# Making Q and K two batches ahead, and dealing the first batch's pieces from two lists

## The chip, the cores and the metric

The kernel runs on one core of one Trainium2 chip. The time is device microseconds of one execution. Three runs of the kernel before are shown: 2144.08, 2147.13 and 2149.2 us, median 2147.13. A core has engines with a queue each: TensorE (PE, its weight loads shown as PEld), VectorE (DVE), ScalarE (ACT), GpSimd (POOL) and SyncE (SP), which here only issues DMAs.

## What is computed

One transformer layer in float32 with post-norm: 8 sequences ("batches") of 1024 rows, width 256, 16 heads of 16, a hidden layer of 1024.

```python
def attention(x):                       # x: (8, 1024, 256)
    Q, K, V = (split_heads(x @ W.T + b) for W, b in ((Wq, bq), (Wk, bk), (Wv, bv)))
    scores = einsum('bhqd,bhkd->bhqk', Q, K) / sqrt(16)
    scores = scores + prior_lambda * gaussian_mask(1024)
    out = einsum('bhqk,bhkd->bhqd', softmax(scores), V)
    return merge_heads(out) @ Wo.T + bo

def ffn(x):
    h = bitlinear(x, w_fc) + gate * (x @ v.T @ fast_b.T @ u.T)
    return bitlinear(relu(h) ** 2, w_proj)     # bitlinear: weights to -1, 0, 1 times a row's mean

x = layernorm(x + attention(x))
out = layernorm(x + ffn(x))
```

## The kernel before

**Groups.** The whole attention is a loop over 512 groups (`for g in range(-LEAD, total + 1)`), 64 to a batch. One group works on two heads' pairs of one block of 128 rows. Its fixed part, in PE's order: the scores transposed for the exps (`exp_scores`, L761, into a tile `e`), some pieces of other work, the scores for the row maxima 12 groups later (`max_scores`, L665, tile `s`), the weighing of the values by the exps of the group before (`weigh`, L791), and matmuls that put the prior into the next `e` (`prior_scores`, L742) where the block lies near the diagonal. DVE reduces each `s` to row maxima (L677), ACT takes the exps (L776), and `e` and `s` share three buffers in PSUM (`se`). The first 12 groups, numbered -12 to -1 (the lead), only take maxima and make what batch 0 needs.

**Pieces.** All else is cut into pieces, each a tuple of cost, function, room in the two halves of the one PSUM bank `misc`, and a test whether it may run. A piece issues its matmuls at once and returns a function that empties the bank, issued after the scores of the maxima. In these texts they are called
- T: two transposes of x (`transpose_x`, L558), eight to a batch; after the fourth the second half of x is loaded into the same tile
- V: a block of the values (`values`, L584), eight to a batch
- Q: a quarter of Q or K of one half of the heads, c = 0 or 1 (`queries_keys`, L611), sixteen to a batch. Every second one is followed on ACT by a cast into the single buffer `two` (L630), a subtraction on POOL (L631), and `write_parts` (L201 to L206), SP's DMAs that write the pair to DRAM (`parts_k`, `parts_q`)
- P, t, L, H, O: output projection, transposes, low rank, hidden layer and output of the feed-forward, in four chunks, 68 to a batch
- weight pieces of batch 0: `prepare_v` (L419, reads `v_sb`), `prepare_fc` (L445, L460, L493, L494) and `prepare_proj` (L531, L537); they make the ternary weights on POOL, and `rows` leaves POOL's low-rank factors in `ones_low`, which L494 turns.

**Which pieces in which batch.** `jobs_of(b)` makes the list for batch b: Q of c = 1 of this batch; T, V and Q of c = 0 of the next one; the feed-forward of the batch before; less the last `KEPT` = 8 pieces, which go to the next batch. 100 pieces in a steady batch. In batch 0 there is no feed-forward, and the weight pieces are mixed with those of batch 1 by `spread`. The lead holds 14 pieces: V of batch 0 and six of the Q pieces of its c = 1.

**Dealing.** In each group the loop takes pieces from the head of the list while there is room in `misc`, the head is ready, and the costs so far (`filled`) are at most 0.75; past that only when the batch is behind (`spare`, the groups left less those that the list still needs), judged more strictly in groups `near` the diagonal. In batch 0 it deals evenly by count instead (`behind`).

**Queues.** An order over all instructions of an engine is fixed at the end, so each engine, SP too, works in the order of the program text. `fill_stack(G)` (L316) is eight SP DMAs that bring Q and K of one group of four heads from DRAM back into the operand tiles `st_k` and `st_q`; it is called every 16 groups, one group of heads ahead, and for G = 1 in group -2. `load_later` (L349 to L353) follows it there and loads `v_sb`, `fast_b`, `u`, the gate and `bo`. `set_max` writes the row maxima to DRAM and back into `st_q` (L702, L709).

Of the kernel before, what the change touches and what calls it, by code (L numbers as in the profile page):

```python
# [37 lines left out]
LEAD = 12  # L38
# [5 lines left out]
def tile_postln_layer(  # L44
# [42 lines left out]
    p2 = ctx.enter_context(tc.tile_pool(name="p2", bufs=2))  # L87
    epool = ctx.enter_context(tc.tile_pool(name="epool", bufs=4))
    dpool = ctx.enter_context(tc.tile_pool(name="dpool", bufs=2, space=bass.MemoryType.DRAM))
    first = len(nc.cur_bb.bb.instructions)  # L90
    before = ExitStack()
    ps_0 = before.enter_context(tc.tile_pool(name="ps_0", bufs=8, space=bass.MemoryType.PSUM))
# [98 lines left out]
    parts_of, made = {}, {}  # L191

    def new_parts(name, b, c):
        parts_of[name, b, c] = dpool.tile(
            [P, 4, L], F32, tag=f"parts_{name}", name=f"parts_{name}_{b}_{c}"
        )
        return parts_of[name, b, c]
# [234 lines left out]
    def prepare_fc(half):  # L432

        n = NHC // 2
        st = {}

        def first():
            w = p1.tile([P, n, D], F32, tag="hi", name=f"fc_{half}")
            nc.sync.dma_start(w, w_fc[ts(half, n * P), :].rearrange("(c p) d -> p c d", p=P))
            st["w"] = w  # L440
            st["uT"] = p1.tile([R, HALF], F32, tag="x1T", name=f"uT_{half}")
            pus = [misc(f"pu_{half}_{k}") for k in range(2)]
            for k, pu in enumerate(pus):
                for i in range(2):
                    nc.tensor.matmul(  # L445
                        pu[:R, ts(i, P)],
                        u_sb[:, n * half + 2 * k + i, :],
                        ident,
                        start=True,
                        stop=True,  # L450
                    )

            def empty():
                for k, pu in enumerate(pus):
                    nc.scalar.copy(st["uT"][:, ts(k, D)], pu[:R, :])

            return empty

        def factor(i, out):
            nc.tensor.matmul(out, st["uT"][:, ts(i, P)], fb_sb, start=True, stop=True)  # L460

        def second():
            pf = misc(f"pf_{half}")[:, :R]
            factor(0, pf)
            return lambda: tern(0, pf)

        def tern(i, pf):
            w, hc = st["w"][:, i, :], n * half + i
            sc = s_fc[:, hc : hc + 1]
            scales(sc, w, D)  # L470
            ternary(w, sc, f"fc_{half}_{i}")
            full = p1.tile([P, R], F32, tag="lowf", name=f"lowf_{half}_{i}")
            nc.scalar.copy(full, pf)

            def rows():

                inv = p2.tile([P, 1], F32, tag="inv", name=f"inv_{half}_{i}")
                nc.vector.reciprocal(inv, sc)
                nc.gpsimd.tensor_scalar(full, full, inv, gate_c, op0=ALU.mult, op1=ALU.mult)
                low = ones_low[:, 1, :].rearrange("p (a b c r) -> p a b c r", a=2, b=2, c=2)  # L480
                for k in range(2):
                    src = full.unsqueeze(1).to_broadcast([P, 2, R])
                    nc.gpsimd.tensor_copy(low[:, k, 0].bitcast(F32R), src)
                    nc.gpsimd.tensor_sub(low[:, k, 1], src, low[:, k, 0])
                st["rows"] = i

            defer(1, rows)

        def piece(i):
            pw = misc(f"pw_{half}_{i}")  # L490
            pl = misc(f"pl_{half}_{i}")
            for dc in range(NDC):
                nc.tensor.transpose(pw[:, ts(dc, P)], st["w"][:, i, ts(dc, P)], ident)  # L493
            nc.tensor.transpose(  # L494
                pl[:, :P], ones_low[:, 1, :], ident
            )
            if i + 1 < n:
                factor(i + 1, pl[:, P : P + R])

            def empty():  # L500
                at = ts(n * half + i, P)
                nc.scalar.copy(wfT[:, :, at], pw.rearrange("p (c h) -> p c h", h=P))
                nc.scalar.copy(lowT[:, at], pl[:, :P])
                if i + 1 < n:
                    tern(i + 1, pl[:, P : P + R])

            return empty

        return [(0.5, first, 2), (0.3, second, 1)] + [
            (0.5, lambda i=i: piece(i), 2, lambda i=i: st.get("rows") == i) for i in range(n)  # L510
        ]

    def prepare_proj(i):
# [887 lines left out]

    over = []

    def first_x(b, main):

        for f, n in zip(first_chunk[b][0], (-8, -2)):
            main[n] = with_(f, main[n])
        return main

    def jobs_of(b):  # L1410


        qk = queries_keys(b, 1, misc)
        load, early_xv, ahead = [], [], []
        if b + 1 < B:
            load = [(0.0, lambda: load_x(b + 1, 0), 0)]
            xs, vs = transpose_x(b + 1, misc), values(b + 1, misc)
            early_xv, ahead = xs[:4] + vs[: NB // 2], xs[4:]
            ahead = ahead + queries_keys(b + 1, 0, misc) + vs[NB // 2 :]
        if b + 1 < B:  # L1420
            first_chunk[b] = chunk(b, 0, misc)
        if b == 0:
            main = [(0.3, prepare_v, 1)] + [u for i in range(2) for u in prepare_fc(i)]
            main += [u for i in range(D // P) for u in prepare_proj(i)]
            side = ahead[:12] + early_xv[4:] + ahead[12:]
            return load + qk + early_xv[:4], first_x(b, spread(main, side, 0.05, 0.9))
        old = [over[k : k + 2] for k in range(0, len(over), 2)] or [[]] * 4
        if ahead:
            t, q, v = ahead[:4], ahead[4:12], early_xv[4:] + ahead[12:]

            lead = [t[0], t[1], q[0], t[2], q[1], t[3], q[2], q[3], v[4], q[4], q[5]]
            at_end = [[q[6], q[7]], [v[5], v[6]], [v[7]], []]
            main = v[:4] + feed_forward(b - 1, misc, lead, at_end)
            t = early_xv[:4]
        else:

            old_o = old[2] + old[3]
            t, old[2:], lead = [()] * 4, [[], []], [qk[6], qk[7], *old_o]
            main, qk = feed_forward(b - 1, misc, lead), qk[:6]
            load = [(0.0, f, 0) for k in (2, 3) for f in (ends[k]["load"], ends[k]["bias"])]  # L1440
            for f, n in zip((ends[0]["load"], ends[0]["bias"]), (-8, -2)):
                main[n] = with_(f, main[n])
        t = [list(u for u in (k,) if u) for k in t]
        jobs = load + [qk[0], *old[0], qk[1], *old[1], *qk[2:4]]

        jobs += [*old[2], *t[0], qk[4], *t[1], *old[3], *t[2], qk[5], *t[3], *qk[6:]]
        over[:] = main[-KEPT:] if b + 1 < B else []
        main = main[:-KEPT] if b + 1 < B else main
        return jobs, first_x(b, main) if b + 1 < B else main

# [48 lines left out]
        *e0["H"][4:],  # L1501
    ]
    rest, es = None, {}
    jobs = [u for part in jobs_of(0) for u in part]

    v_first, qk_first, jobs[:7] = values(0, misc), jobs[1:7], jobs[:1]
    early = [u for two in zip(v_first, qk_first) for u in two] + v_first[6:]
    for g in range(-LEAD, total + 1):

        now = g  # L1510
        if g == -8:
            split_prior()
        if g == -2:
            fill_stack(1)
            load_later()
        if 0 <= g < total and g % per_batch == 0:
            if g:
                assert not jobs
                jobs = [u for part in jobs_of(g // per_batch) for u in part]
        if g == total - 7:  # L1520

            old, jobs = jobs, []
# [29 lines left out]
        if g < 0:  # L1552

            n = g + LEAD + 1 - (done >= QSTEP - 1)
            upto = 14 * n // (LEAD - 1)
            if halves == 2:
                work += [early.pop(0)[1] for _ in range(len(early) - 14 + upto)]
        elif g < total:
            left = per_batch - 1 - g % per_batch
            if g == 0:  # L1560
                among = len(jobs)
            if g < per_batch:

                behind = len(jobs) > among * (1 - (g + 1) / (per_batch - 3))
            else:

                spare = left - groups_for(jobs) if g < total - per_batch else 0
            while jobs and halves >= jobs[0][2] and ready(jobs[0]):
                cost = jobs[0][0]
                if g < per_batch:  # L1570
                    if not (cost == 0.0 or behind):
                        break
                    behind = len(jobs) - 1 > among * (1 - (g + 1) / (per_batch - 3))
                elif filled > 0.75 and not (spare < (-1 if near(g) else 2)):
                    break
                elif filled > 0.9 and cost > 0.9 and spare > -4:
                    break
                cost, piece, room = jobs.pop(larger(jobs) if halves == 1 and g >= per_batch else 0)[:3]
                filled += cost
                halves -= room  # L1580
                work.append(piece)
# [103 lines left out]
```

## Time and profile before

| | |
|---|---|
| median of three runs | 2147.13 us |
| the profiled execution, its time | 2146.07 us |
| its span | 2144.3 us |
| PE busy | 2073.6 us (97%), weight loads 1200.6 us (56%) |
| DVE, ACT, POOL busy | 73%, 67%, 43% of the span |
| DMA | 193.55 MB, mean 90 GB/s |
| mean granted clock of TensorE | 0.994 |
| group 0 of the loop begins | 61.3 us |
| batches 0, 1, 2 to 6, 7 take | 242.4, 254.2, 253.7 to 253.8, 253.6 us |
| after the loop (from 2080.4) | 63.9 us |

Batches are told apart in the trace by the starts of the L761 matmuls, four to a group. A busy PE is not PE at its peak, since a matmul's record also holds time in which it stands in the array's pipeline. A wait is shown in brackets behind an instruction: how long its engine stood idle before it, and what ended this. "SPq" is SP's issue of a DMA, not the transfer.

### The profile page before, as it was taken

What the parts mean: (1) busy time and instruction counts of PE and PEld (TensorE: products, weight loads), DVE (VectorE), ACT (ScalarE), POOL (GpSimd) and SP (SyncE); (2) the same over time, 40 slices, a digit from 0 to 9 for tenths busy, and PEclk for the clock granted to TensorE, in tenths of its full rate; (3) what the DMA queues carried; (4) which work ended last, traced back from release to release, by engine and by line L of the source; (5) the groups of instructions that cost most, each with busy time, mean ns of one, the idle gap of its engine ahead of it and who ended that gap; (6) DMA issues with size and microseconds to landing.
All of it is one profiled execution on the core that took longest, in us unless ns stands there. A gap on an engine that the chain in (4) does not pass through costs nothing.

```text
span 2144.3 us, 38970 instructions
## 1 busy us (share of the span) xinstructions
PE 2073.6 (97%) x14200; PEld 1200.6 (56%) x14200; DVE 1568.2 (73%) x2909; ACT 1440.2 (67%) x2155; POOL 917.2 (43%) x1075
## 2 busy tenths in 40 slices
PE   6999999999999999999999999999999999999997
PEld 3444445555555555556555555555555555555657
DVE  6777777777777777777777777777777777777736
ACT  2566666766777667667777767677676766766754
POOL 5044332344324453345533445335543445455444
PEclk9999999999999999999999999999999999999999
DMA  6423334223433124423233223422343321422010
GB/s 192 124 76 112 77 88 143 68 62 78 124 103 107 56 60 121 137 73 84 72 133 110 76 70 99 132 86 58 78 124 120 90 70 49 138 74 56 23 47 20
DMA packets 110725, 193.55 MB, mean 90 GB/s; under 512 B 21149, under 2 KB 50253, under 8 KB 110533
## 3 DMA queue, kind: packets, MB, share of 16 engines
q1 hardware_dynamic: 109116, 189.48, 31.3%
q8 instruction: 112, 1.84, 0.4%
q10 hardware_dynamic: 1416, 1.58, 0.2%
q14 instruction: 81, 0.66, 0.1%
HBM read 105.19 MB, written 85.69 MB: 89 GB/s over the span
## 4 chain that ended last, share of the span: by engine, by line
PE 80%; DVE 11%; POOL 3%; DMA 3%; issue 2%; ACT 1%; SPq 0%; DVEq 0%; POOLq 0%; ACTq 0%
PE e L761 22%; PE av L791 19%; PE s L665 16%; DVE junk L677 8%; PE misc L1065 5%; PE misc L611 4%; PE misc L1100 4%; PE misc L584 2%; PE misc L991 2%; PE e L742 1%; PE misc L1072 1%; DVE st L949 1%; DMA parts_k<-twok 1%; PE misc L1025 1%; PE misc L558 0%
## 5 line engine op out<-in xcount | busy, mean ns | idle before, releaser
L677 DVE CUSTOM_DVE_ANT_0 junk<-s,wide 128x1024 f32<-128x1024 f32 x1024 | 1249.1, 1220 | 484.1 <-PE s L665 440.5
L776 ACT ACTIVATE exp<-e 128x1024 f32<-128x1024 f32 x1024 | 1027.6, 1024 | 549.2 <-PE e L761 371.3
L761 PE MATMUL e<-st_q,st_k 66*128 66x512 f32 (+1 forms) x2048 | 618.0, 423 | 0.7 <-DMA st_q<-rows 0.4
L791 PE MATMUL av<-exp,v 128*17 128x512 f32 x4096 | 539.8, 598 | 0.0
L761 PEld LDWEIGHTS e<-st_q,st_k 66*128 66x128 f32 (+1 forms) x2048 | 344.0, 189 | 292.8 <-ACT exp L776 95.3
L665 PE MATMUL s<-st_k,st_q 64*128 64x512 f32 x2048 | 393.9, 446 | 40.1 <-DVE pm L677 25.9
L665 PEld LDWEIGHTS s<-st_k,st_q 64*128 64x128 f32 x2048 | 165.3, 185 | 172.3 <-DVE pm L677 88.6
L775 DVE TENSOR_TENSOR e<-e,wide 128x372 f32<-128x372 f32 (+2 forms) x376 | 190.1, 506 | 38.2 <-PE e L761 35.7
L1083 POOL TENSOR_TENSOR rl<-rl 128x512 f32<-128x512 f32 x112 | 116.7, 1042 | 234.1 <-ACT hi L1082 221.1
L791 PEld LDWEIGHTS av<-exp,v 128*17 128x17 f32 x4096 | 68.1, 95 | 185.7 <-issue 184.3
L742 PEld LDWEIGHTS <-ident_q 96*32 96x32 bf16 x2112 | 64.3, 97 | 162.9 <-issue 159.0
L1085 POOL TENSOR_TENSOR lo<-rl,hi 128x512 fp32r<-128x512 f32 x112 | 143.8, 1284 | 8.8
L1120 POOL TENSOR_TENSOR r<-r,sp_row 128x256 f32<-128x256 f32 x56 | 41.1, 734 | 212.0 <-ACT r L1119 212.0
L594 POOL TENSOR_TENSOR v<-v,bv_row 128x256 f32<-128x256 f32 x64 | 44.0, 689 | 191.9 <-ACT v L593 191.9
L1065 PE MATMUL misc<-xhi,wfT 128*128 128x256 f32 x448 | 117.0, 284 | 0.4 <-ACT fullq L626 0.2
L1065 PE MATMUL misc<-xlo,wfT 128*128 128x256 f32 x448 | 115.0, 280 | 0.0
L1100 PE MATMUL misc<-wpT,lo 128*128 128x256 f32 x448 | 112.0, 282 | 2.6 <-POOL lo L1085 2.6
L1100 PE MATMUL misc<-wpT,hi 128*128 128x256 f32 x448 | 114.3, 288 | 0.0
L631 POOL TENSOR_TENSOR twok<-fullk,twok 128x512 fp32r<-128x512 f32 x30 | 38.6, 1287 | 145.3 <-ACT twok L630 143.6
L1078 ACT ACTIVATE rl<-misc,s_fc 128x256 f32<-128x256 f32 x224 | 94.0, 475 | 0.9 <-POOL lo L1085 0.9
L1065 PEld LDWEIGHTS misc<-xhi,wfT 128*128 128x128 f32 x448 | 84.4, 188 | 10.6 <-ACT fullk L626 2.4
L1100 PEld LDWEIGHTS misc<-wpT,lo 128*128 128x128 f32 x448 | 85.3, 190 | 6.7 <-POOL lo L1085 3.2
(233 smaller groups left out, 2351.9 us busy)
## 6 DMA issues: line engine op xcount, KB each, us to landing
st_k<-parts_k SPq DMA_DIRECT2D x128, 256.0 KB
st_q<-parts_q SPq DMA_DIRECT2D x124, 256.0 KB
parts_k<-twok SPq DMA_DIRECT2D x60, 512.0 KB
parts_q<-twoq SPq DMA_DIRECT2D x64, 256.0 KB
parts_q<-twoq SPq DMA_DIRECT2D x30, 512.0 KB
x<-in_L_attn_x_dram SPq DMA_DIRECT2D x16, 512.0 KB
raw_o<-avs SPq DMA_DIRECT2D x248, 32.0 KB
rec<-back SPq DMA_DIRECT2D x30, 256.0 KB
```

The source lines that it names most:

```text
L611: nc.tensor.matmul(pt, wT[name][:, dc, ts(c, P)], xT[:, dc, ts(2 * half + k, D)], start=(dc == 0), stop=(dc == NDC - 1),)
L665: nc.tensor.matmul(pair[a][:, kh, :], stack["q", s, pr, a][rows, ts(blk, P)], stack["k", s, pr, a][rows, ts(kh, HALF)], start=True, stop=True,
L677: nc.vector.tensor_tensor_reduce(out=junk, in0=t.rearrange("p k n -> p (k n)"), in1=wide[:, LEFT - P * blk : LEFT - P * blk + L], scale=1. ...
L761: nc.tensor.matmul(t[:, a, :], stack["k", s, pr, a][rows, ts(blk, P)], stack["q", s, pr, a][rows, ts(h, HALF)], start=not by_pe, stop=True ...
L775: nc.vector.tensor_add(part, part, add.to_broadcast([P, 2, hi - lo]))
L776: nc.scalar.activation(e, t.rearrange("p a n -> p (a n)"), AF.Exp)
L791: nc.tensor.matmul(av[32 * j : 32 * j + HD + 1, :], v_bufs[b % 2][:, blk, g * HG + j, : HD + 1], es[j // 2][:, ts(j % 2, HALF)], start=(n ...
L1065: nc.tensor.matmul(ph, wfT[:, dc, ts(hc, P)], st[k2][:, dc, :], start=(dc == 0 and k2 == "xhi"), stop=False,)
L1078: nc.scalar.activation(rl[:, ts(k, n)], ph, AF.Relu, scale=s_fc[:, hc : hc + 1])
L1083: nc.gpsimd.tensor_mul(rl, rl, rl)
L1085: sub(lo, rl, hi.bitcast(F32))
L1100: nc.tensor.matmul(py, st[k][:, hc, ts(i, P)], wpT[:, hc, :], start=(hc == 0 and k == "hi"), stop=(hc == NHC - 1 and k == "lo"),)
```

## The change

- `jobs_of(b)` now makes T and all 16 Q pieces of batch b + 2, and V of batch b + 1, beside the feed-forward of b - 1. Batch 6 so has no T and Q, batch 7 no T, Q and V; batch 6 leaves 12 pieces to batch 7 where the others leave 8.
- The `parts` tiles in DRAM come from a pool with six buffers for each name, where there were two.
- Batch 0 deals from two lists: `prepare` (weight pieces) and `side` (T, Q of batch 1, V of batch 1, T and Q of batch 2). Both are spaced evenly by count; after a weight piece a side piece still goes into the same group if the costs stay under 1.2 (1.1 near the diagonal). `prepare_v` is the first piece of group 0 (it was dealt in group 7).
- The lead now holds 20 pieces: all eight Q pieces of batch 0's c = 1 and four T pieces of batch 1. x of batch 1 is loaded when the loop starts (it was in group 0).
- A weight piece of `prepare_fc` waits one group more after `rows`.
- In later batches the rule for a second piece changes: -0.5 for -1 near the diagonal, no second piece past 0.4 while more than three groups are spare, and a fixed `spare` in the last batch.

```diff
-        parts_of[name, b, c] = dpool.tile(
+        parts_of[name, b, c] = dparts.tile(
...
-                st["rows"] = i
+                st["rows"], st["at"] = i, now
...
-            (0.5, lambda i=i: piece(i), 2, lambda i=i: st.get("rows") == i) for i in range(n)
+            (0.5, lambda i=i: piece(i), 2, lambda i=i: st.get("rows") == i and now > st["at"] + 1) for i in range(n)
...
-        qk = queries_keys(b, 1, misc)
...
+        v = values(b + 1, misc) if b + 1 < B else []
+        load, t, q0, q1 = [], [], [], []
+        if b + 2 < B:
+            load, t = [(0.0, lambda: load_x(b + 2, 0), 0)], transpose_x(b + 2, misc)
+            q0, q1 = queries_keys(b + 2, 0, misc), queries_keys(b + 2, 1, misc)
...
-            side = ahead[:12] + early_xv[4:] + ahead[12:]
-            return load + qk + early_xv[:4], first_x(b, spread(main, side, 0.05, 0.9))
+            side = transpose_x(1, misc) + queries_keys(1, 0, misc) + queries_keys(1, 1, misc)
+            return first_x(b, main, (-8, -2)), side + load + v + t + q0 + q1
...
+            lead = [t[4], t[5], q0[0], t[6], q0[1], t[7], *q0[2:]]
+            at_end = [q1[2:4], q1[4:6], q1[6:], []]
+            main = q1[:2] + feed_forward(b - 1, misc, lead, at_end)
+            t, v[6:] = [[u] for u in t[:4]], [v[6:]]
...
+            old += [[]] * (4 - len(old))
+            jobs = load + [v[0], *old[0], v[1], *old[1], *v[2:4]]
+            jobs += [*old[2], *t[0], v[4], *t[1], *old[3], *t[2], v[5], *t[3], *v[6]]
+        kept = KEPT if b + 2 < B else KEPT + 4
...
-    v_first, qk_first, jobs[:7] = values(0, misc), jobs[1:7], jobs[:1]
-    early = [u for two in zip(v_first, qk_first) for u in two] + v_first[6:]
+    early = [u for two in zip(values(0, misc), queries_keys(0, 1, misc)) for u in two]
+    early, side = early[:8] + side[:4] + early[8:], side[4:]
...
+        if g == -LEAD:
+            load_x(1, 0)
...
+        elif g < per_batch:
+            part = 1 - (g + 1) / (per_batch - 3)
+            while prepare and halves >= prepare[0][2] and ready(prepare[0]):
+                if filled > 0.1 or len(prepare) <= n_prepare * part:
+                    break
...
+            while side and halves >= side[0][2] and ready(side[0]):
+                cost = side[0][0]
+                if cost and (len(side) <= n_side * part - 3 or filled + cost > (1.1 if near(g) else 1.2)):
+                    break
...
-                elif filled > 0.75 and not (spare < (-1 if near(g) else 2)):
+                if filled > 0.75 and not (spare < (-0.5 if near(g) else 2)):
+                    break
+                elif filled > 0.4 and spare > 3:
                     break
```

## The prediction

> **What bounds the kernel now.** I read the batches first, as eight windows of the core's time (columns: stretch, us, then busy time of PE, weight loads, DVE, ACT and POOL, the granted clock, the DMA share and GB/s); the batches with numbers 0, 1, 5 and 7 are these:
>
> ```profile
> 61.30:303.73 242.43, 224.83 (x1518) 113.41 (x1513) 183.93 (x331) 153.68 (x220) 79.83 (x117) 0.99 0.31 84
> 303.73:557.90 254.17, 249.48 (x1706) 141.26 (x1701) 188.53 (x347) 175.22 (x260) 100.46 (x112) 1.00 0.33 93
> ...
> 1319.20:1573.00 253.80, 252.22 (x1758) 146.37 (x1752) 189.01 (x351) 179.29 (x269) 111.35 (x125) 1.00 0.33 94
> ...
> 1826.80:2080.41 253.61, 245.87 (x1721) 143.67 (x1715) 170.66 (x330) 173.88 (x250) 124.54 (x143) 1.00 0.25 69
> ```
>
> Batch 0 takes 242.4 us though PE stands idle for 17.6 us of it; the later ones take 253.8 with PE idle for 1.6. No other engine is near its limit. To price a moved piece I then took single groups, in the same columns: an empty one without and one with matmuls of the prior, one with a Q piece, one with Q and a transpose of x, one with two H pieces and the prior, one with an O piece.
>
> ```profile
> 289.14:292.70 3.56, 3.10 (x23) 1.29 (x17) 3.15 (x6) 2.05 (x2) 0.00 (x0) 1.00 0.02 5
> 296.38:300.05 3.67, 3.43 (x30) 1.60 (x24) 3.05 (x6) 2.05 (x2) 0.00 (x0) 1.00 0.03 9
> 303.73:307.37 3.64, 3.64 (x26) 1.87 (x21) 2.60 (x5) 2.41 (x3) 0.00 (x0) 1.00 1.05 225
> 1397.22:1401.10 3.88, 3.88 (x27) 2.04 (x22) 2.92 (x6) 2.62 (x4) 0.00 (x0) 1.00 0.00 0
> 1437.53:1441.59 4.06, 4.06 (x39) 2.74 (x34) 3.44 (x8) 2.52 (x4) 0.35 (x1) 1.00 0.03 8
> 1445.68:1449.40 3.72, 3.72 (x30) 2.21 (x24) 3.20 (x8) 2.50 (x3) 3.03 (x4) 1.00 1.04 226
> ```
>
> An empty group has a **floor** of 3.55 us (3.68 with the prior), from the three score buffers going round PE, DVE and ACT. A Q piece adds only 0.09; the next piece pays in full (+0.24 for the transpose). The rows fit: group = the larger of the floor and 2.77 (+0.13 prior) + pieces, at Q, V or P 0.865, T 0.23, L 0.48, H 0.6, O 0.95, row maxima 0.11. So 0.78 us of each group is free, and batch 0 leaves most of it unused. The Trainium skill (Perfetto Trace Analysis, section Identifying the Most-Contended Engine) says that matmul busy time is no measure of headroom. The page's 97% for PE would promise nothing for a refilled batch 0, the 0.09 us of the Q row promises nearly 0.8 per filled group; the rows decide, and the sum uses them alone.
>
> Last I read what PE waits for in batch 0, and the queue at its start.
>
> ```profile
> PE misc L494 <- POOL ones_low L484: 4.7, 6, 1.7
> ```
> ```profile
> 193.71 0.33 PE L494 MATMUL misc<-ident,ones_low 128*128 128x128 f32 x1 [1.67 <-POOL ones_low L484]
> ...
> 195.77 2.07 PE L761 MATMUL e<-st_q,st_k 66*128 66x512 f32 x4
> ...
> 197.64 1.61 PE L611 MATMUL misc<-xT,wqT 128*128 128x256 f32 x4
> ```
> ```profile
> 55.86 0.48 SPq L316 DMA_DIRECT2D st_k<-parts_k  x1
> ...
> 60.86 0.59 SPq L349 DMA_DIRECT2D v_sb<-in_L_ffn_v_dram  x1
> ...
> 65.51 0.38 SPq L201 DMA_DIRECT2D parts_k<-twok  x1
> ```
> ```profile
> 335.64 0.62 ACT L630 CAST twoq<-fullq 128x512 fp32r<-128x512 f32 x1 [1.34 <-DMA parts_k<-twok]
> ```
>
> Weight pieces wait for POOL. After the longest wait four e matmuls took 2.07 us instead of 1.20: the granted clock was 0.5 from 195.4 to 198.8, worth about 1.6 us. The Trainium skill (TensorE: Matmul & The Clock Gate, section What's actually happening) puts the half clock behind an idle window of about 3.4 us; here 1.67 us of wait came before it. By the page short waits would cost only themselves (4.7 us to be won from the weights); the row makes it 6.3, and I take the row. The last fence shows a cast that waits for the single `two` buffer, until the write of the pair before has landed.
>
> **The change, part by part.** The loop's rule, followed group by group with the readiness tests, gives the old order as the trace has it, and for the new one these tables' sums (old in brackets): batch 0 237.9 (234.1), batch 1 247.0 (246.3), each of 2 to 5 251.4 (250.3), batch 6 238.2 (250.3), batch 7 247.9 (251.1). The old batches took 8.3, 7.9, 3.5 and 2.5 more than their tables (0, 1, 2 to 6, 7): waits, which I carry over except where named.
>
> (1) Lead: x of batch 1 is loaded when the loop starts, in SP behind the fills that end at 40.4; a 512 KB write issued at 41.22 landed 2.7 us later, one at 41.65 3.6 later. The first T piece stands in group -8, which PE reaches at about 41.6, so x, at 43.1 to 44.9, is late. DVE's reduction pair of the next group stood at 43.00 and needs scores behind T: +2.0, from 0.5 to 3.5. No gain: reductions pace these groups at 1.38 each.
>
> (2) Groups 0 and 1: `prepare_v` moves from group 7 to 0, so PE wants v_sb at 62.4 and not at 89. The trace's completion events put the eight fills' landings at 59.4 to 68.1, one per 1.24 us, and v_sb's at 68.3, right behind them. Now the pair of K's second half is finished in group -3, ahead of fill_stack(1) in SP's order: V at 53.63 on PE, ACT held until 56.07 by the rows' DMA, then 0.37 + 0.47 + 0.62, POOL 1.29: 58.8. With two writes in front, fills start near 60 instead of 55.86 and v_sb lands near 73.4. PE waits 11 us; behind v_sb's matmuls stand T, the scores for DVE and all that follows. Two floor groups 7.2 + 11 + about 1 for the half clock, against 8.5 now: +10.7. Bounds: 0 (it lands in time) and +13.5 (two half-speed windows). Both shift with (1).
>
> (3) Batch 0 from group 2: table +3.9, for 26 more pieces; with one group more between rows and weight piece the 6.3 of L494 go. x's second half is loaded in group 41 and used in 42, 3.7 us later: +0.5. Q pieces run through 44 to 53 across the fill of group 48: the write of the cast in 49 queues behind some 13 us of fills, and the cast in 51 waits as in the last fence: +2.5 (0 to 4). Sum +0.6.
>
> (4) Batch 1: table 247.0, with the neighbours' 3.5 of waits and 1.5 for a cast behind the fill of group 16: 252.0, so -2.2 (-4 to +2).
>
> (5) Batches 2 to 5: the same 100 pieces, of which the last two groups get at most one: +1.1 by the table; the cast of group 18 after the one of 16 finds its buffer's write behind the fill: +0.8 (0 to 2). Four times 1.9: +7.6, from -2 to +14.
>
> (6) Batch 6: no transposes and no Q for a batch 8, four pieces more left over: 72 pieces for 100. Table -12.1; single H pieces leave POOL time, so waits fall from 3.5 to 2.5: -13.1 (-8 to -15.6).
>
> (7) Batch 7: eight Q pieces gone, four added, all in groups 0 to 11: table -3.2, and their casts' waits: -3.5 (-2 to -5). The tail is unchanged.
>
> Five more DRAM buffers and the new lists issue nothing. The DMA counts stay; only their order moves.
>
> Sum: 2.0 + 10.7 + 0.6 - 2.2 + 7.6 - 13.1 - 3.5 = **+2.1**. On the profiled execution's 2146.1 that is 2148.2; this execution lies 1.1 below the median of 2147.1 and inside the runs' 2144.1 to 2149.2.
>
> **The rivals.** *The start does not wait*: the small v_sb overtakes the fills and x comes in time. For: no instruction of before waited for either, and v_sb is 16 KB. Against: the completion order above. It takes 9 off (2) and 1 off (1): 2138. *Cast waits in every batch* (slower): runs of Q pieces, 15 to 23 in a steady batch, make a cast every two groups, 7.7 us; once a write needs longer from cast to landing, ACT holds the exps behind it. Group 72 of before shows the price: 4.68 us for a floor of 3.55. Two more per batch in 1 to 5 add 11.3: 2159.5. For: fills keep the queue for 12 us four times a batch; against: eight Q pieces running at 303.7 to 334 met one such wait. *Batch 6 does not shrink*: groups of one H stay near 3.95 through something not in my table, and (6) gives only 3: 2158. Against: the floor of 3.55 in batch 0.
>
> **How the numbers follow.** About 0.2% (4.3 us) is what a measurement tells from no change: same means 2142.8 to 2151.4. The forecast has chance 0.50, with its own range 2143 to 2154 (faster 0.05, same 0.33, slower 0.12 of it); the start that does not wait 0.25 (0.22 faster, 0.03 same); cast waits 0.19 (0.02 same, 0.17 slower); batch 6 0.06, slower. Together faster 0.27, same 0.38, slower 0.35. The range 2137 to 2160 reaches to both rivals and leaves out their outer halves.
>
> **What would show it.** Step (1): PE waits for x in the lead, near 42. (2): PE waits about 11 us for v_sb, with half clock after it. (3): no wait at the ones_low transpose; a cast wait near group 51. (5): batches 2 to 5 at about 255.7. (6): batch 6 near 240.7. (7): batch 7 near 250. The forecast is wrong if PE passes the v_sb matmuls at once, or if casts wait over 3 us per batch.

## The result, and the profile after

| | before | after |
|---|---|---|
| median, four runs of each side by side | 2148.11 us (2144.08 to 2149.20) | 2235.34 us (2235.14 to 2236.79) |
| ratio | | 1.0416, 95% interval 1.0403 to 1.0429 |
| span of the profiled execution | 2144.3 | 2233.5 |
| mean granted clock of PE | 0.994 | 0.976 |
| PE, DVE, ACT, POOL busy | 2073.6 us; 73%, 67%, 43% | 2105.1 us (94%); 70%, 64%, 41% |
| group 0 of the loop begins | 61.3 | 66.8 |
| batch 0, 1 | 242.4, 254.2 | 272.2, 259.0 |
| batches 2 to 5, each | 253.7 to 253.8 | 266.2 to 266.9 |
| batch 6, 7 | 253.8, 253.6 | 250.7, 254.7 |
| after the loop | 63.9 | 64.3 |

The changed kernel is 4.2% slower. The forecast was 2148.2 us with a range of 2137 to 2160. The spans differ by 89.2 us, and the table says where: 5.5 in the lead, 29.8 in batch 0, 4.8 in batch 1, 50.8 in batches 2 to 5, 1.1 in batch 7, 0.4 at the end, less 3.1 in batch 6.

The view of the batches as windows (stretch, us, then busy time of PE, weight loads, DVE, ACT and POOL, granted clock, DMA share, GB/s), for batches 0, 1, 5, 6 and 7 after the change:

```profile
66.84:339.00 272.16, 245.01 (x1614) 130.53 (x1608) 183.68 (x330) 169.50 (x258) 94.20 (x128) 0.94 0.39 118
339.00:598.00 259.00, 250.47 (x1707) 140.73 (x1701) 188.70 (x348) 175.78 (x260) 100.31 (x112) 0.99 0.34 95
...
1396.90:1663.80 266.90, 256.82 (x1758) 148.35 (x1752) 189.53 (x352) 178.99 (x268) 111.10 (x124) 0.99 0.32 89
1663.80:1914.50 250.70, 240.44 (x1660) 136.96 (x1652) 189.06 (x350) 164.18 (x230) 94.50 (x110) 0.99 0.22 54
1914.50:2169.20 254.70, 243.43 (x1710) 141.72 (x1703) 171.14 (x331) 170.42 (x243) 122.88 (x142) 0.99 0.22 56
```

Batch 5 shows the same 1758 PE entries as before, and its other engines are busy as long as before. PE now stands idle there for 10.1 us where it was 1.6. This waiting is 8.5 of the 13.1 us by which the batch grew; the other 4.6 are the same entries taking longer. In batch 0 it is 27.2 us, with a clock of 0.94.

One of these waits had been foreseen. The timeline of PE at the start of group 0 (start, us, engine, line, what, and in brackets the idle time before it and who ended it):

```profile
66.84 1.20 PE L762 MATMUL e<-st_q,st_k 66*128 66x512 f32 x4
78.84 1.00 PE L420 MATMUL misc<-ident,v_sb 16*128 16x16 f32 x4 [10.80 <-DMA v_sb<-in_L_ffn_v_dram]
```

PE waits 10.8 us for `v_sb`. Within this wait the clock fell to half and stayed there for 17 us, 9.2 of them behind the wait:

```profile
70.99:88.06 17.07, 9.02 (x30) 4.25 (x34) 4.52 (x11) 2.76 (x5) 0.00 (x0) 0.50 0.73 179
```

The large one had not. In each of batches 2 to 5, group 52 takes 11.3 to 12.6 us for a floor of 3.55. The timeline of batch 3 around it, first SP's queue (group 48 begins at 1058.05, group 52 at 1074.61):

```profile
1061.29 0.39 SPq L202 DMA_DIRECT2D parts_k<-twok  x1
...
1063.71 0.38 SPq L1115 DMA_DIRECT2D out_dram<-r  x1
1064.13 0.52 SPq L317 DMA_DIRECT2D st_k<-parts_k  x1
...
1068.54 0.59 SPq L317 DMA_DIRECT2D st_q<-parts_q  x1
1069.18 0.59 SPq L977 DMA_DIRECT2D x<-in_L_attn_x_dram  x1
...
1074.72 0.34 SPq L830 DMA_DIRECT2D den<-sums  x1
```

then the engines that need what stands at the end of that queue:

```profile
1076.55 1.40 POOL L983 TENSOR_TENSOR x<-x,bo_row 128x256 f32<-128x256 f32 x2 [10.50 <-DMA x<-in_L_attn_x_dram]
...
1078.25 0.55 DVE L835 RECIPROCAL den<-den 128x64 f32<-128x64 f32 x1 [3.41 <-DMA den<-sums]
...
1081.01 0.43 DVE L950 BATCH_NORM_STATS2 st<-r 128x6 f32<-128x256 f32 x1 [2.21 <-POOL r L1002]
...
1081.57 1.19 DVE L678 CUSTOM_DVE_ANT_0 junk<-s,wide 128x1024 f32<-128x1024 f32 x1
...
1082.82 1.29 PE L666 MATMUL s<-st_k,st_q 64*128 64x512 f32 x4 [5.84 <-DVE pm L678]
```

Read it from the end. PE waits 5.84 us for DVE's row maxima. DVE had nothing against them; they stand, in its order, behind the statistics of a norm, and those wait for POOL's residual `r`. POOL reaches `r` late since it waited 10.5 us, in its order, for a 256 KB piece of x to add a bias to. That piece was issued at 1069.18, behind the eight DMAs of `fill_stack` (2 MB). And the fill went out at 1064.13, 6.1 us after group 48 began, since two writes stood ahead of it on SP, each waiting for POOL: a K pair, and the store of a finished chunk. Before, the same queue read

```profile
998.03 0.50 SPq L316 DMA_DIRECT2D st_k<-parts_k  x1
...
1007.10 1.70 SPq L812 DMA_DIRECT2D raw_o<-avs  x4
...
1014.26 0.40 SPq L1114 DMA_DIRECT2D out_dram<-r  x1
```

with group 48 at 1001.61: the fill 3.6 us ahead of the group, the store 16 us behind the fill. The new lists end the O pieces of the chunk in group 45, where it was 47, and put a K pair into groups 46 and 47, where there was none. So both writes come in front of the fill. The P pieces that need x now stand in groups 50 and 51, where it was 52 and 53, so x is also wanted two groups sooner. This I shall call the order theory: SP, POOL and DVE each work in order, and one held entry on SP becomes, three queues on, a wait of PE.

### The profile page after: what moved, and what is told of

It reads as the page before. It is cut to its first block, busy times and chain, and to the rows that moved or that the text cites. A ratio compares the mean times of both kernels' runs of the same rounds, so it can differ in the third digit from the quotient of the medians.

```text
span 2233.5 us, 38927 instructions
## 1 busy us (share of the span) xinstructions
PE 2105.1 (94%) x14200; PEld 1219.3 (55%) x14200; DVE 1571.0 (70%) x2909; ACT 1439.6 (64%) x2155; POOL 915.9 (41%) x1075
## 4 chain that ended last, share of the span: by engine, by line
PE 63%; DVE 11%; DMA 3%; POOL 2%; ACT 1%; issue 1%; SPq 1%; DVEq 0%; POOLq 0%; ACTq 0%
PE e L762 17%; PE av L792 15%; PE s L666 13%; DVE junk L678 8%; PE misc L1066 4%; PE misc L1101 3%; PE misc L612 3%; PE misc L992 2%; PE misc L585 1%; DMA x<-in_L_attn_x_dram 1%; PE misc L1073 1%; PE e L743 1%; DVE st L950 1%; DVE xlo L1030 1%; SPq L317 1%
## 5 line engine op out<-in xcount | busy, mean ns | idle before, releaser
L762 PE MATMUL e<-st_q,st_k 66*128 66x512 f32 (+1 forms) x2048 | 624.6, 427 | 8.0 <-DVE pm L678 5.5
L792 PE MATMUL av<-exp,v 128*17 128x512 f32 x4096 | 547.9, 607 | 0.0
L666 PE MATMUL s<-st_k,st_q 64*128 64x512 f32 x2048 | 403.3, 451 | 78.7 <-DVE pm L678 61.1
L666 PEld LDWEIGHTS s<-st_k,st_q 64*128 64x128 f32 x2048 | 172.3, 188 | 205.9 <-DVE pm L678 98.9
L1066 PE MATMUL misc<-xhi,wfT 128*128 128x256 f32 x448 | 122.2, 295 | 0.7 <-ACT fullq L627 0.2
```

Source lines behind the costliest of these rows:

```text
L666: nc.tensor.matmul(pair[a][:, kh, :], stack["q", s, pr, a][rows, ts(blk, P)], stack["k", s, pr, a][rows, ts(kh, HALF)], start=True, stop=True,
L762: nc.tensor.matmul(t[:, a, :], stack["k", s, pr, a][rows, ts(blk, P)], stack["q", s, pr, a][rows, ts(h, HALF)], start=not by_pe, stop=True ...
L792: nc.tensor.matmul(av[32 * j : 32 * j + HD + 1, :], v_bufs[b % 2][:, blk, g * HG + j, : HD + 1], es[j // 2][:, ts(j % 2, HALF)], start=(n ...
L1066: nc.tensor.matmul(ph, wfT[:, dc, ts(hc, P)], st[k2][:, dc, :], start=(dc == 0 and k2 == "xhi"), stop=False,)
```

## The experiments

Times below are of one profiled execution each, beside a run of the kernel before at 2145 to 2147 us, except where an interval is given. Single times that differ by a few us tell little: 17 runs of the kernel before, in one sitting, lie between 2141.2 and 2151.8 us. The readings below rest on the batches and waits of each trace.

**The order theory: fill first.** Call of `fill_stack` moved one group up, ahead of that group's pair writes:

```diff
-        if g > 0 and 2 * g % PER_G == 0 and 2 * g // PER_G + 1 < B * NG:
-            fill_stack(2 * g // PER_G + 1)
 ...
             exps[1]()
+        G, r = divmod(2 * (g + 1), PER_G)
+        if G > 0 and r == 0 and G + 1 < B * NG:
+            fill_stack(G + 1)
```

> The changed kernel, with the fill of the next stack put one group earlier in the program, behind the last e matmul that reads the slot and ahead of the writes of that group's pair. Order theory (SP issues in order; a pair's write that waits for POOL holds back the fill behind it, and the den and x1 loads behind the fill land too late for DVE and POOL): the fills of batches 2 to 5 are issued 3 us ahead of group 48's start instead of 6 us after it, the 5.8 us wait of the s matmul in group 52 and the half clock behind it go, batches 2 to 5 fall from 266.4 to 256 to 258 each, batch 0 by some 8; the whole near 2190. Cast theory (casts wait for the one buffer `two` whose write is late): the writes now stand behind the fill and the casts wait longer; batches 2 to 5 stay at 266 or grow, the whole 2235 to 2245. Dealing theory (more pieces in a batch than its groups hold): no change, 2235.

Measured 2202.7 us. The fills of group 48 go out at -4.0 us, batches 2 to 5 take 258.2 to 258.6, batch 0 268.4. For these batches the dealing and cast theories fall. But the whole is 13 above what the order theory said, and batch 1 grew by 7.5 to 266.5. Its trace holds a second test that I had not planned. In the changed kernel x for that chunk was loaded ahead of the fill (at 533.44, the fill at 534.28) and batch 1 had no stall in group 51. Here the fill has overtaken it; SP's and DVE's lines:

```profile
530.17 0.76 SPq L317 DMA_DIRECT2D st_k<-parts_k  x1
...
535.96 0.59 SPq L977 DMA_DIRECT2D x<-in_L_attn_x_dram  x1
```
```profile
548.33 0.43 DVE L950 BATCH_NORM_STATS2 st<-r 128x6 f32<-128x256 f32 x1 [5.43 <-POOL r L1002]
```

and group 51 takes 10.8 us. So it is not the lateness of the fill itself that counts, but that of the small load behind it.

**Fill later.** The opposite move, for group 48 only:

```diff
-        if g > 0 and 2 * g % PER_G == 0 and 2 * g // PER_G + 1 < B * NG:
-            fill_stack(2 * g // PER_G + 1)
+        f = g - 2 if g % per_batch == 50 else g
+        if f > 0 and 2 * f % PER_G == 0 and ... and not (f == g and g % per_batch == 48):
+            fill_stack(2 * f // PER_G + 1)
```

> The changed kernel, with the fill of group 48 of each batch put two groups later in the program, behind the raw_o, sums, den and x1 transfers; its own readers start in group 52. Order theory: what made the stall was the small loads behind the fill, so with them ahead of it the stall of group 52 goes although the fill is no earlier: batches 2 to 5 at 256 to 259, the whole near 2192. Readers theory (the s matmuls of group 52 wait for the late fill itself): batches 2 to 5 stay at 266 or grow by up to 4 each, the whole 2235 to 2250.

Measured 2199.7 us; batches 2 to 5 take 258.2 to 258.6. SP's queue in batch 3, where group 48 begins at 1046.67:

```profile
1052.32 0.38 SPq L1115 DMA_DIRECT2D out_dram<-r  x1
1052.74 0.51 SPq L977 DMA_DIRECT2D x<-in_L_attn_x_dram  x1
...
1055.78 0.44 SPq L830 DMA_DIRECT2D den<-sums  x1
1056.32 0.50 SPq L317 DMA_DIRECT2D st_k<-parts_k  x1
```

The fill is now 9.6 us late, 3.5 more than in the changed kernel, and the stall is gone: a fill that is earlier and a fill that is later remove the same 8 us, 32 in the four batches. The readers theory falls for these batches; in batch 0 PE does wait 3.0 us in group 52 for the late fill itself. Both leave 258.4, 4.6 above the kernel before.

**v_sb sooner.**

```diff
         if g == -8:
             split_prior()
+            load_later()
         if g == -2:
             fill_stack(1)
-            load_later()
```

> The changed kernel, with v_sb and the other small inputs loaded in group -8 instead of -2, ahead of the fill of the second stack. If v_sb is late only because it stands behind that fill: the 10.8 us wait of the v_sb matmul goes, with it most of the 17 us of half clock, and groups 0 and 1 take 8 to 9 us instead of 21 to 22; the whole falls by 12 to 15, to 2221. Rival (the start waits for the fill, the bands or x as well, v_sb is only the first): a wait of 5 us or more stays in groups 0 to 2 and the whole falls by less than 6.

Measured 2222.8 us, 12.5 less. PE passes `v_sb` at once behind the e matmuls, groups 0 and 1 take 9.9 us together for 21.5, batch 0 takes 260.4. Nothing else of that size had been waiting behind the load.

```profile
65.95 1.20 PE L762 MATMUL e<-st_q,st_k 66*128 66x512 f32 x4
67.08 0.61 PE L420 MATMUL misc<-ident,v_sb 16*128 16x16 f32 x4
```

**What makes the lead long.** The transposes last among its pieces:

```diff
-    early, side = early[:8] + side[:4] + early[8:], side[4:]
+    early, side = early + side[:4], side[4:]
```

> The changed kernel, with the four transposes of x of batch 1 put last among the pieces of the lead instead of ninth to twelfth. If the 5.5 us by which the lead grew came from x, which is not there in time, and the half clock behind that wait: the lead ends at 62 to 63 us instead of 66.8 and PE waits for x no more. If four more pieces in the lead cost that much by themselves: it ends at 66 to 67. The K pair of the second half is done two groups sooner, so the fill and v_sb come up to 3 us sooner as well; the whole 2228 by the first, 2233 by the second.

Measured 2238.8 us: the lead ends at 67.2, not at 62 to 63, and batch 0 grew to 276.2. PE waits for x no more, and the lead is no shorter. My first reading of the lead, that the transposes wait for x, was wrong; the four runs at the end of this section come back to it.

**One part of the change alone, in the kernel before.**

```diff
-                st["rows"] = i
+                st["rows"], st["at"] = i, now
 ...
-            (0.5, lambda i=i: piece(i), 2, lambda i=i: st.get("rows") == i) for i in range(n)
+            (0.5, lambda i=i: piece(i), 2, lambda i=i: st.get("rows") == i and now > st["at"] + 1) for i in range(n)
```

> The kernel before, with one part of the change alone: a weight piece waits one group more behind the rows that POOL writes for it. My step 3 gave this part 6.3 us of gain in batch 0 (4.7 of waits at the ones_low transpose and 1.6 of half clock): batch 0 at 236 to 238 for 242.4, the whole 2141 to 2143 for 2147. Rival: the pieces only move to later groups, whose other work they meet, and what the waits cost comes back: batch 0 at 241 to 243, no difference.

Median 2146.59 us for 2146.47 (12 and 17 runs), ratio 1.000 (0.9988 to 1.0011). No wait at the `ones_low` transpose is left, yet the whole is the same, as the rival says; a gain of 6.3 us lies outside the interval, one of 2.5 does not. Whether the cost comes back in the way the rival has it is not shown. In the one execution with a trace, batch 0 took 239.9 for 242.4 and batch 1 256.3 for 254.2, but batch 7, which this part does not touch, took 7.1 more as well. Also, this kernel does not compute the layer: in group 47 two pieces of `prepare_proj` now stand together, and the second transposes weights that have not been made ternary yet. It stands for the time alone, and with a wait of its own, 1.8 us for POOL in group 48.

**The pair writes off SP.** POOL issues them itself, behind its subtraction:

```diff
-def write_parts(name, t, two, half, rows=slice(0, P)):
+def write_parts(name, t, two, half, rows=slice(0, P), queue=nc.sync):
 ...
-                write_parts(name, t, two, half)
+                write_parts(name, t, two, half, queue=nc.gpsimd)
```

> The changed kernel, with the writes of the Q and K pairs issued by POOL, behind the subtraction that they wait for, on its own DMA queue; SP no longer waits for POOL, and the program's order of fills and small loads is that of the changed kernel. Order theory: the fills of batches 2 to 5 go out 3 us ahead of group 48, the stall in group 52 goes (batches 2 to 5 at 257 to 259), and the casts that waited for writes behind a fill (group 19 of batch 1, group 52 of batch 0) wait no more: batch 1 at 253 to 255, batch 0 at 262 to 266; the whole 2185 to 2192. Bandwidth theory (the late writes and loads share the DMA engines with 2 MB of fill, whatever the queue): the two cast waits stay at 2.7 us and more and the whole is 2198 to 2204, as with the fill moved. If POOL's issuing costs engine time that its bias and residual work needs: over 2210.

Measured 2238.8 us: neither of the first two numbers, and above the 2210 of the third. Batches 2 to 5 got longer (267.3 to 269.4). The timeline of batch 3 says why:

```profile
1058.20 0.82 POOL L202 DMA_DIRECT2D parts_k<-twok  x1 [0.30 <-POOL twok L632]
...
1059.80 2.44 POOL L961 TENSOR_SCALAR r<-r,mv,rstd 128x256 f32<-128x256 f32 x2
...
1062.27 0.40 SPq L1115 DMA_DIRECT2D out_dram<-r  x1
1062.89 0.50 SPq L317 DMA_DIRECT2D st_k<-parts_k  x1
```

Group 48 begins at 1054.70. The pair's write is off SP, but the store was the last of the two to be released, and POOL, which now spends 1.6 us on the write's two DMAs, scales the chunk for it 1.9 us later in the group: the fill goes out at +8.2. My first account had named the pair alone. The other half of the expectation failed too: the casts behind fills still wait (3.3 us in group 17 of batch 1, until 401.95, for a write that POOL issued from 393.2 to 394.6), on a queue with no fill in it. So here a second queue did not shield a write from 2 MB in the first.

**The store out of the way**, alone and with the POOL writes:

```diff
                 norm_apply(r, r, mv, st["rstd"])
-                nc.sync.dma_start(
-                    out[b, ts(c, CT * P), :].rearrange("(t p) d -> p t d", p=P), r
-                )
+                to = out[b, ts(c, CT * P), :].rearrange("(t p) d -> p t d", p=P)
+                defer(2, lambda: nc.sync.dma_start(to, r))
```

> The changed kernel, with the store of each finished chunk put two groups later in the program, so that it no longer stands between the K pair's write and the fill of group 48. POOL ends the pair's subtraction 2.4 us before the chunk's last scaling, for which the store waits. Two writes (either holds the fill; the later one, the store, decides, and the pair's write is next): the fill of batches 2 to 5 goes out near +4.2 us instead of +6.1, the x1 and den loads land 1.9 us sooner, the stall of group 52 shrinks to 5 to 6 us but stays: these batches at 263 to 265, the whole 2225 to 2230 (group 4 of batch 7, which waits behind a store as well, gives 4 more: 2221 to 2226). Pair alone (my first account: only the pair's write holds the fill): nothing changes in batches 2 to 5, 266. Store alone: the fill goes out at -3 us and the stall goes, 258.

> The pair writes issued by POOL, and the store two groups later: nothing that waits for POOL is left ahead of the fill of group 48. Order theory: the fill goes out at -3.3 us and the stall of group 52 goes: batches 2 to 5 at 257 to 259, for 267 to 269 with the POOL writes alone; group 4 of batch 7 loses 4 us; the whole 2190 to 2197. If POOL's issues or the shared DMA engines made the stall of the run with POOL writes: 266 and more, the whole above 2225.

Alone: 2233.7 us. The fill goes out at +4.2 to +4.9, as two writes would have it, yet the stall is almost as long as ever (group 52 of batch 3 takes 11.0 us, batches 2 to 5 265.7 to 266.6): its length does not follow the fill's lateness, I had that wrong. POOL still waits 10.2 us for x:

```profile
1077.98 1.42 POOL L983 TENSOR_TENSOR x<-x,bo_row 128x256 f32<-128x256 f32 x2 [10.22 <-DMA x<-in_L_attn_x_dram]
```

Batch 7 fell by 3.5. Both together: 2198.1 us, the fill at -4.0, batches 2 to 5 at 258.3 to 258.7. It takes both writes to free the fill, and POOL's issues do not make the stall. Here x stands right behind the fill, and does no harm, since both are early:

```profile
1048.10 0.59 SPq L317 DMA_DIRECT2D st_q<-parts_q  x1
1048.73 1.51 SPq L977 DMA_DIRECT2D x<-in_L_attn_x_dram  x1
```

What the length does follow can be read from all these traces. The times are us behind the start of group 48, in batches 2 to 5:

| | fill goes out | x issued | POOL begins on x | group 52 takes |
|---|---|---|---|---|
| before (P pieces two groups later) | -3.6 | 13.6 | 16.4 to 17.3 | 3.6 |
| changed | 6.1 | 11.1 to 11.9 | 18.5 to 19.9 | 11.3 to 12.6 |
| fill first | -4.0 | 6.1 | 11.8 to 13.0 | 4.1 to 4.4 |
| fill later | 9.6 to 10.7 | 6.1 | 9.1 to 10.5 | 4.1 |
| POOL writes | 8.2 | 13.3 | 20.6 to 21.8 | 13.4 to 14.6 |
| store later | 4.2 to 4.9 | 9.9 to 10.6 | 18.1 to 19.1 | 10.8 to 11.8 |
| POOL writes and store later | -4.0 | 1.1 to 1.4 | 9.9, without a wait | 4.1 |

In each of the twelve stalls group 52 takes 7.2 us less than the time at which POOL begins on x, within 0.1. So x sets the length, not `den` and not the fill.

**Batch 6.** Fill later, and without the rule that keeps groups light while there is time:

```diff
-                elif filled > 0.4 and spare > 3:
-                    break
```

> The changed kernel with the fill of group 48 two groups later, and without the new rule of the dealing that lets a group with 0.4 of work take no second piece while more than three groups are to spare. It acts in batches 1, 6 and 7. Theory (the last P pieces of batch 6, dealt in groups 54 and 55, hold the o tile, so that SP stands at its next load and the rows behind it come late): with the P pieces in groups 45 and 46 the wait for the rows in group 55 goes and groups 55 and 56 take 7 to 8 us together, where they took 12.4; the batch's last nine groups stand empty, so batch 6 takes 246 to 250, against 249.6. Rival (the rows are late for another reason, such as the fill of group 48): the wait stays.

Measured 2198.6 us, batch 6 250.8 for 249.6. In the changed kernel's list of waits the two lines of the case are

```profile
SPq L845 <- PE misc L992: 10.8, 1, 10.8
```
```profile
PE e L762 <- DMA st_q<-rows: 2.4, 1, 2.4
```

(who waited for whom: us in total, times, longest). SP stands 10.8 us at the next load of `o` until the last P piece has read the tile, and the row maxima behind it come late. With the P pieces in groups 45 and 46 both lines are gone and groups 55 and 56 carry no wait. The theory holds, and it buys nothing: the last nine groups of the batch stand empty and the earlier ones are fuller.

**Three mends together.** POOL writes, `load_later` in group -8, and `second` of `prepare_proj` ready only when `now > st["at"] + 3`, three groups behind its load:

> The changed kernel with three mends at once: the pair writes issued by POOL, v_sb loaded in group -8, and the reduction over w_proj held three groups behind its load. If the waits are those that the trace names and add up: group 34 of batch 0 loses its 6 us, groups 0 and 1 some 12, and the whole is that of the POOL writes alone less 17 to 19, near 2170. That is still 22 above the kernel before, which would leave the lead (+5), the steady batches (4.5 each) and batch 0 as the rest. If the waits only move on to the next late transfer: less than 10 below the POOL writes alone.

Measured 2232.8 us, 6.0 below the POOL writes alone: the waits moved on. ACT in group 0, and in group 49:

```profile
74.33 0.62 ACT L632 CAST twoq<-fullq 128x512 fp32r<-128x512 f32 x1 [6.54 <-DMA parts_k<-twok]
...
267.53 0.62 ACT L632 CAST twok<-fullk 128x512 fp32r<-128x512 f32 x1 [4.46 <-DMA parts_q<-twoq]
```

The K pair's write, issued by POOL from 64.5 to 65.9 beside a fill that SP issued from 60.8 to 65.7, has not landed before 74.3.

**All that helped.** `load_later` in group -8, fills of group 48 and of group 32 of batch 0 two groups later, the store two groups later, no rule at 0.4:

> The changed kernel with all that helped: v_sb in group -8, the fill of group 48 in each batch and of group 32 in batch 0 two groups later, the store two groups later, no rule at 0.4. If the waits add: the run without that rule (2198.6) less 11.8 (start), 6.3 (group 34 of batch 0, whose reduction waits for w_proj behind a fill), 4.3 (group 4 of batch 7): 2176. If a mended wait only moves on to the next late transfer: above 2186.

Measured 2182.5 us, between the two. Batch 0 falls from 267.8 in the run without the rule to 250.5 (17.3 of the 18.1 expected). Batch 7 did not fall (257.1). Without the rule at 0.4 its stall stands in group 3 and no longer in 4, already in that run (8.0 us, the batch 256.4): POOL waits for a load of x for the last chunks behind the fill, as in group 52; the later store does not touch that. No version of the changed kernel comes near the kernel before; the best took 2181.3 us.

**The lead once more.** From that kernel: the transposes out of the lead; then also x of batch 1 loaded in group -2; or only 14 pieces in the lead; or both.

```diff
-    early, side = early[:8] + side[:4] + early[8:], side[4:]
 ...
-                if cost and (... filled + cost > (1.1 if near(g) else 1.2)):
+                if cost and (... filled + cost > 1.2):
```
```diff
-        if g == -LEAD:
-            load_x(1, 0)
 ...
             fill_stack(1)
+            load_x(1, 0)
```
```diff
-    early = [u for two in zip(values(0, misc), queries_keys(0, 1, misc)) for u in two]
+    vs, qk = values(0, misc), queries_keys(0, 1, misc)
+    early, side = [u for two in zip(vs, qk[:6]) for u in two] + vs[6:], qk[6:] + side
```

> The kernel of the sum, with the four transposes of x left out of the lead and dealt in batch 0 instead, where a group with the prior may then take 1.2 of work for 1.1. If four more pieces cost the lead its 5 us by themselves: the lead ends at 61 to 62 us instead of 66 to 67, batch 0 grows by 1 to 2, and the whole falls by 3 to 4. If the lead is long for another reason (x's transfer beside the fills, half clock): it stays at 65 or more.

> The kernel without transposes in the lead, with x of batch 1 loaded in group -2, behind the fill, instead of at the loop's start. If x's 512 KB, which stand ahead of the pair writes of the lead, make the casts wait and so the lead long: the lead ends at 61 to 63 us, for 67.9. If the two Q pieces more in the lead do: 66 to 68. What x costs at its new place shows in groups 0 to 3 and is another matter.

> The kernel without transposes in the lead, with the 14 pieces that the lead of the kernel before holds (8 V, 6 Q and K), x of batch 1 loaded at the loop's start as before. If the two Q pieces more make the lead long: it ends at 61 to 63 us. If x's load does: 66 to 68.

> Both: 14 pieces in the lead and x of batch 1 in group -2. The lead is then that of the kernel before but for five small loads in group -8: 60 to 62 us by either theory. If it stays at 65 or more, the five small loads are the cause in these kernels and nothing is learnt of the changed one.

| in the lead | ends at | batch 0 | whole |
|---|---|---|---|
| 20 pieces, x at the loop's start (that kernel) | 66.8 | 250.5 | 2182.5 |
| 16 pieces, x at the loop's start | 67.9 | 265.1 | 2195.9 |
| 16 pieces, x in group -2 | 61.0 | 275.5 | 2196.0 |
| 14 pieces, x at the loop's start | 63.6 | 258.3 | 2181.3 |
| 14 pieces, x in group -2 | 60.6 | 261.4 | 2184.8 |

The transposes cost the lead nothing (67.9 without them). But dealt in batch 0 they cost it 14.6 us where I had expected 1 to 2: PE waits for x there, 3.7 us in group 3 and 5.3 in group 41. x's 512 KB ahead of the pair writes cost the lead 3.0 with 14 pieces and 6.9 with 16; the two Q pieces more cost 0.4 without x and 4.3 with it. Neither is the cause alone. With 16 pieces and x ahead, a cast waits for the write of the pair before:

```profile
48.61 0.62 ACT L631 CAST twoq<-fullq 128x512 fp32r<-128x512 f32 x1 [4.36 <-DMA parts_k<-twok]
```

With x in group -2 this wait is 1.1 us, and with 14 pieces 0.5 or nothing, so the cast explains the longest lead in part and the 3.0 not at all. The 3.0 and the 0.4 are no more than chance can make: five runs with the lead of the changed kernel ended it between 66.5 and 69.9. Loading x later does not pay: batch 0 grows by as much or more.

## Why the prediction was wrong

**What bounds the kernel, and the table of pieces**: right. Of the 64 groups of batch 3 with the fill later, 48 agree with the table within 0.2 us. The table is not where the 87 us are.

**(1) Lead, +2.0; +5.5.** The bound was +3.5. I had x late for its own reader, and PE did wait for it in the lead, 1.6 us, and a cast 1.7. What my sum left out was x on its way past the pair writes, and the two Q pieces more. In the last four runs they cost 7.3 together, 3.9 of it only where both are there. Which waits make up the rest is not shown.

**(2) Groups 0 and 1, +10.7; +12.9.** Confirmed in place, cause and size: 10.8 us of wait for 11, and the run with the earlier load takes it away. The wait was not what fell short: without it the two groups took 9.9 us in that run, 3.4 of them at half clock, where I had counted two floor groups, 7.2.

**(3) Batch 0 from group 2, +0.6; +16.9.** One term was missing and two were too small. The reduction over `w_proj` waits 5.5 us in group 34, since its load stands behind the fill of group 32; in the kernel with all that helped, where that fill is later, the wait is gone. The cast wait that I put at 2.5 near group 51 was 7.3 in group 52, and DVE stood there for `den` as long, 6.5. PE's wait for the second half of x in group 42 was 1.6 for 0.5. The waits at the `ones_low` transpose went as I had said, and 51 of the 64 groups agree with the table within 0.2; but alone, in the kernel before, that part made no difference to the whole.

**(4) Batch 1, -2.2; +4.8.** The cast wait behind the fill of group 16 came, at 2.7 us for the 1.5 that I allowed, and group 19 took 4.9 more than the table.

**(5) Batches 2 to 5, +7.6; +50.8. This is the step that failed.** It had a cast behind a fill, at 0.8 a batch, and put the loads behind the fill of group 48 at nothing. I asked of the moved pieces which cast would wait for which buffer, and of the fills whether their own readers would get them in time. I did not write down SP's queue around each fill. It would have shown a pair write and a store, both waiting for POOL, in front of the fill of group 48, and behind the fill x, for which POOL waits 10.5 to 11.9 us and in the end PE 5.8 to 7.2. The runs give 32 of the 43 missing us to this: they go when the fill is moved up, when it is moved down, and when both writes are moved away. The other 11 (2.7 a batch) stand in none of these; three different mends all end at 258.2 to 258.7. In the trace they are spread over single groups, such as 0.3 to 0.4 in each group of L with Q and 0.5 in the pair of H behind it. No run tests that.

**(6) Batch 6, -13.1; -3.1.** The shorter list was there, but 5.8 went to groups 55 and 56 through P pieces that came late, as shown, and beside them PE waited 6.9 us for row maxima, in 20 places. My third rival had the number (-3) for a reason that does not hold: 18 of the 21 groups with one H and no larger piece took 3.5 to 3.7 us.

**(7) Batch 7, -3.5; +1.1.** The same pattern in group 4: a store ahead of the fill, 4.6 us. With the store later batch 7 takes 251.2, -2.4 against the kernel before.

**The rivals.** The cast waits, my slower case, were the right kind of mechanism in the wrong place: casts waited 14 us in all, 10 of it in the lead and batch 0, where I had reckoned with two in every batch. It gave 2159.5, and the time lay 76 above. The start that does not wait fell with the 10.8 us. Only step (2) had a small load that is late behind a fill; I did not ask the same of the fills in the loop.

## What to carry to other kernels

A piece that is moved takes its DMAs along. Write down the issuing queue before and after around every large transfer, and ask of each entry in front of it what it waits for, and of each entry behind it, however small, who needs it and what stands behind that reader on its own in-order engine. In the changed kernel the fills' own readers never waited from group 0 on; the reader of the 256 KB behind one did.

To test such a chain, move the large transfer in both directions: if sooner and later both remove the stall, its own lateness is not what counts; then look for what stands behind it. And a wait removed alone, or a second queue, can prove little until the rest of the chain is gone: `v_sb` sooner paid in full here, but the store or the POOL writes alone left the stall standing.

## What the hardware showed that I had not expected

A write on a queue of its own was not shielded: the last 512 KB of a K pair, issued by POOL beside 2 MB from SP, took over 8 us from the end of the issue to the cast that waited for it, where the median of POOL's K writes in that run was 3.9 us from issue to landing. A DMA issue by POOL took 0.54 to 0.96 us of POOL's own time (150 issues, median 0.73).

The half clock came behind short waits as well. Behind the 5.84 us stall of group 52, and behind the 2.42 us wait in batch 6, the granted clock was 0.5 for the same 6.83 us:

```profile
1081.34:1088.17 6.83, 5.35 (x18) 2.43 (x19) 4.45 (x9) 3.41 (x6) 2.63 (x3) 0.50 0.37 115
1880.06:1886.89 6.83, 6.61 (x26) 4.20 (x26) 2.85 (x6) 3.52 (x5) 1.41 (x2) 0.50 0.13 41
```

The Trainium skill (TensorE: Matmul & The Clock Gate, section What's actually happening) asks for an idle window of about 3.4 us before the clock drops; the first row agrees with it, the second does not.
